# Reordering the turn between two steps of a graph layer on one NeuronCore: keys, laws, a guess, a product and a proof change places

## The chip, the cores and the metric

The kernel runs on one core of a Trainium2 chip. The metric is the device time of one execution, in microseconds (us). Five engines work side by side, each through its own queue in order: TensorE (PE; PEld is its weight load), VectorE (DVE), ScalarE (ACT), GpSimd (POOL), and SyncE (SP), which here only issues DMAs. GpSimd issues the indirect DMAs (gathers). "Clock" is the share of TensorE's full clock that was granted. The time before is 1377.8 us, the median of three runs (1377.0, 1377.8, 1383.6).

## The reference

Inputs are 3327 nodes with 256 features, a sparse weighted graph S, small weights, and a layer norm. With N = 3327 and two steps:

```python
def _top_p_attention(X, W1, W2, W3):
    q = X @ W1.T @ W2.T
    k = X @ W3.T
    probs = jax.nn.softmax(q @ k.T / TAU, axis=-1)
    ...
    keep_sorted = cs - sp < TOP_P          # cs: running sum of the sorted row
    ...
    A = probs * mask
    return A / jnp.maximum(A.sum(-1, keepdims=True), 1e-12)
R = S + jnp.eye(N); R = R / R.sum(-1, keepdims=True)
for n in range(STEPS):                      # 2
    A = _top_p_attention(Xa, W1, W2, W3)
    Xf = R @ Xf
    Xa = A @ Xa
    Z = Z + Xf @ U1[n].T + Xa @ U2[n].T
h = X + Z
return layernorm(h) * ln_g + ln_b           # and x + this, X = relu(layernorm(x))
```

So each step needs, for every node, a softmax row over all nodes, of which only the largest entries that hold 90% of the mass are kept, a product with the features, and a sparse graph product. The second step's attention reads the first step's result of all nodes.

## The kernel before, in words

Rows are cut into 26 tiles of 128 (tile 25 has 127 rows that count). The program is one function, `guess_graph_layer`; a slower exact search stands behind a branch and isn't run here.

For each tile and step the work is:

- **weights** (L581): project queries (L522), four chunks of logits on PE (L599) into two PSUM banks of the pool `ps_l`, each chunk taken out by ScalarE as an exponential with its sum (L603; the last chunk L607 and L609).
- **the guess** of the cut (L611 to L713): ScalarE sums up (L619 to L624), scans the row of 3328 values in passes called `ja` (L632), small VectorE instructions stand between the passes (L684, L685 after the second pass of the second step; L698 to L706 after the third), then POOL's (L675 to L711), then ScalarE's last one (L713). It needs the tile's "law", moments of its logits: `project` (L524, L531, L537, L540 to L544) for tiles 0 to 2, and `laws` (L548) for tiles 3 to 25 in the second step: eight groups on PE and VectorE (L556, L559 to L562), then two ScalarE and ten POOL instructions (L567 to L575) for all of them.
- **settle** (L722): VectorE masks the row (L728), takes the largest values (twenty L733, then L740 and L742 in turns, L747 to L752) and cuts the row (L762, or in two pieces L759 for the first and last tile). 
- **Sums** (L795): PE transposes the row (L808), ScalarE copies it out (L810), PE multiplies it with the features (L822); ScalarE scales the result in the first step (L831).
- **spread** (L1077): the graph product, six matmuls (L908, twelve records in the profile) of gathered rows, then an addition on VectorE (L1089, L1090), and in the first step a store to the table `vx`, from which the second step gathers (L900).
- **first_end** (L916, first step): transpose (L473, L476), two products (L921) with copies (L922, L924), and `prep` (L480): queries and keys of the second step (L484, copies L492 and L493). **finish** (L931) ends the second step.
- **prove** (L770): VectorE shows for a step that all guesses were good enough; `proof` (L954) runs it for the second step, and then a matmul (L958) makes a flag.

Between the steps stand `moments` (L503; L506, L508 to L512), the laws, and the first tiles' weights. The second step's first logits can only be made when the keys of tile 25 are there.

The pools `ps_a` (sums) and `ps_r` (graph products, `pz`) have one PSUM bank each, `ps_l` and `ps_t` (all else) two each.

The order on PE, ScalarE and VectorE, and on GpSimd from the second step on, is the order of the text (a chain of dependencies made at the end, L1193 and the lines below); only GpSimd's order before that, and SyncE's, is left to the tile framework. The text's order comes from strings: for each tile index i from -1 to 27 there are seven slots, and each letter of a slot's string advances one generator by a piece. `m` is the guess of tile i+1, `n` the one that was `m` before, `d` and `c` settle of tile i and of the one before, `s` spread, `w` and `q` weights, `e` first_end, `l` laws, `g` gathers, `f` finish, `v` proof. What a generator still holds at the end of the index is run there. `PLAN` is the usual string, `BEGIN`, `OPEN` and `LAST` those of the first and last indices. Before the change:

```python
    OPEN = {-1: ("llcmss", "lnms", "lwwnfd", "lcmdsssggggg", "fmgdswqdf", "llmdf", "lmwfdm"),
            0: ("cmssggg", "nms", "wwnfd", "cmdsss", "fdsmgwqdf", "mdf", "mwd"),
            1: ("cmss", "nms", "wwnfd", "cmdsssgggg", "fdsmwqdf", "mgdf", "mwdg")}
```

Of the kernel before, what the change touches and what calls it, by code (L numbers as in the profile page):

```python
# [9 lines left out]
F32 = mybir.dt.float32  # L10
# [8 lines left out]
P = 128  # L19
N = 3327  # L20
D = 256
DA = 64
NT = (N + P - 1) // P
# [321 lines left out]
def guess_graph_layer(ctx, tc, x, adj, w1t, w2t, w3t, u1t, u2t, ln_g, ln_b, out, flag):  # L345
# [17 lines left out]
    rows_of = lambda t: min(P, N - t * P)  # L363
# [431 lines left out]
    class Sums:  # L795
# [18 lines left out]
        def sum(self, g):  # L814

            t, k = divmod(g, PARTS)
            if k == 0:
                self.pa = ps_a.tile([P, 2 * D], F32, tag="pa", name="pa")[:, :D]
            eT = self.eT.pop(g)
            for c in range(4 * k, min(4 * k + 4, NT)):  # L820
                j = c % HALF * 2 + c // HALF
                PE.matmul(self.pa, eT[:, c - 4 * k, :], self.xa[:, j, :], start=c == 0, stop=c == NT - 1)  # L822
            if k < PARTS - 1:
                return None
            if self.step:
                return t, (self.pa, self.live.pop((self.step, t))["ra"])
            n = rows_of(t)
            dst = row.tile([P, D], F32, tag="xa", name="xa", bufs=2)
            if n < P:
                V.memset(dst, 0.0)  # L830
            S.activation(dst[:n], self.pa[:n], AF.Copy, scale=self.live.pop((self.step, t))["ra"][:n])  # L831
            return t, dst
# [83 lines left out]
    def first_end(t):  # L916
        aT = transposed(live.pop(("r", t)))
        yield
        pz = ps_r.tile([P, 2 * D], F32, tag="pr", name="pz")
        for c in range(ND):  # L920
            PE.matmul(pz, aT[:, c, :], u2[:, c].rearrange("p n d -> p (n d)"), start=c == 0, stop=c == ND - 1)  # L921
        S.copy(xw[:, t, :], pz[:, D:])  # L922
        sv = row.tile([P, D], F32, tag="sv", name="sv", bufs=2)
        S.copy(sv, pz[:, :D])  # L924
        G.tensor_tensor(sv, sv, x0[:, t, :], ALU.add)
        nc.sync.dma_start(sx[t], sv)
        yield
        yield from prep(aT, t)

# [24 lines left out]
    def proof():  # L954
        prove(1)
        yield
        pf = ps_t.tile([P, 4, P], F32, tag="pt", name="pf")
        PE.matmul(pf[:1, 0, :1], fl, ones, start=True, stop=True)  # L958
        V.tensor_copy(flag, pf[:1, 0, :1])
# [115 lines left out]


    def spread(step, t):  # L1077
        rr = rrs[:, t : t + 1]
# [17 lines left out]
    def refetch(t):  # L1096
        acs[t] = adjp.tile([P, KT, P], F32, tag="ac", name="ac", bufs=2)
        nc.sync.dma_start(acs[t].rearrange("p k r -> p (k r)"), cx[t])
        yield from fetched(vx, t, D)
# [13 lines left out]
             1: ("mdsssbba", "mcdsssbba", "edbawwbp", "msdbga", "mpdea", "dawwq", "emgq")}  # L1113
    OPEN = {-1: ("llcmss", "lnms", "lwwnfd", "lcmdsssggggg", "fmgdswqdf", "llmdf", "lmwfdm"),
            0: ("cmssggg", "nms", "wwnfd", "cmdsss", "fdsmgwqdf", "mdf", "mwd"),
            1: ("cmss", "nms", "wwnfd", "cmdsssgggg", "fdsmwqdf", "mgdf", "mwdg")}
    OPEN[2] = OPEN[3] = OPEN[1]
    fetching = itertools.chain(*(refetch(t) for t in range(NT)))
    LATE = (1, 4)
    BLOCKS = ({}, {1: (0, 1), 2: ()})  # L1120
# [4 lines left out]
    for step in range(2):  # L1125
        sums = Sums(step, live, xw if step else x0, AHEAD[step])

        for i in range(-1, NT + 2):
# [4 lines left out]
            if step == 1 and i == -1:  # L1133
                run(begun[0])
                prove(0)
                for e in es[4:]:
                    G.memset(e[:, N:NP], 0.0)
# [4 lines left out]
                m=measured(step, live[step, i + 1]) if valid(i + 1) else none,  # L1142
                s=spread(step, i - 2 + 2 * step) if valid(i - 2 + 2 * step) else none,
                w=later.pop((step, i + 2), none),
# [4 lines left out]
                b=none if step else product, q=none, v=proof() if step and i == NT else work.get("v", none),  # L1149
                l=laws(range(3, NT)) if step and i == -1 else work["l"] if step and i == 0 else none,  # L1150
            )
            if i >= 0 and valid(i + 3):
                later[step, i + 3] = weights(step, i + 3, live)
                work["q"] = itertools.islice(later[step, i + 3], 2 - step)
            if step == 0 and i >= NT - 2 and i < NT + 1:

                work["w"] = itertools.islice(begun[i - NT + 2], CUT - 1)
            if step == 0 and i >= NT - 3 and i < NT:
                work["q"] = itertools.islice(begun[i - NT + 3], 1)
            if i == -1:  # L1160
                work["w"] = begun[1] if step == 0 else itertools.chain(begun[1], begun[2])
            if step == 0 and i == 0:
                work["w"] = begun[2]
            for k in range(PARTS):
                g = PARTS * (i - 1) + k - LATE[step]
                summing = valid(g // PARTS)
                if step and valid((g + AHEAD[1]) // PARTS):
                    sums.turn(g + (k == 2), min(i, NT - 1))
                for c in ({**OPEN, **LAST} if step else BEGIN).get(i, PLAN[step])[k]:
                    next(work[c], None)  # L1170
# [12 lines left out]
            if step and i < 1:  # L1183
                next(fetching)
            for c in ("lcnwqsepb" if i > -1 else "cnwqsepb") if step else "cmwqsep" + "gb" * (i > 0):
# [55 lines left out]
```

## Time and profile before

| | |
|---|---|
| time, median of three runs | 1377.8 us (1377.0 to 1383.6) |
| the profiled execution | 1380.51 us, its span 1378.8 us |
| busy in the span | PE 1279.0 us (93%), DVE 1188.6 (86%), ACT 1079.2 (78%), POOL 954.0 (69%) |
| mean granted clock | 0.98 |
| last attention product of the first step ends | 772.6 us |
| first cut of the second step (L759) | 815.62 us |
| usual distance between two tiles in the second step | 21.0 us |
| last attention product of all ends | 1365.7 us |

The page cuts the span in 40 slices of 34.5 us; PE's row of busy tenths is 9 nearly all along, with a 7 and a 5 at about 760 to 830 us, the turn between the steps, and the clock's row is 6 and 9 there. Lines of the timeline give start, duration, engine, line of the kernel, operation, output and inputs, shapes, count, and in brackets the idle time before with what ended it. A matmul of 32-bit floats shows as two records. Ends of matmuls are modelled, and POOL's spans are rough.

### The profile page before, as it was taken

Reading aid. Unit: us, or ns where it says so; the run is one execution under the profiler, and the core shown is the slowest. Engines: PE = TensorE matmul, PEld = TensorE weight load, DVE = VectorE, ACT = ScalarE, POOL = GpSimd, SP = SyncE. Lnnn points to the kernel's source line nnn. Section 1 sums busy time; section 2 is a strip of 40 time slices with the busy share of each in tenths; the row PEclk is TensorE's granted clock in tenths of the full one; section 3 lists DMA queues with packets and bytes.
Section 4 is the critical chain, followed back from the end, with each engine's and each line's share of the span. In section 5 each row is a group of like instructions: output and inputs, shape, how many; then the busy total and the mean of one; then the engine's idle time right before and its main releaser. Section 6 shows DMA issues by size and latency. Waiting matters only on the chain.

```text
span 1378.8 us, 22108 instructions
## 1 busy us (share of the span) xinstructions
PE 1279.0 (93%) x6495; PEld 975.2 (71%) x6495; DVE 1188.6 (86%) x3637; ACT 1079.2 (78%) x2368; POOL 954.0 (69%) x1399
## 2 busy tenths in 40 slices
PE   5999999999999999999999759999999999999985
PEld 4535777776777777777777537777776777777774
DVE  6888889998898899999884389999998999999993
ACT  5466687787788788878774589899998999999941
POOL 6312888765777668766664377888888888888832
PEclk9999999999999999999999969999999999999998
DMA  8764454454454454444423112212222122221200
GB/s 275 246 183 146 123 152 132 132 148 117 123 152 121 126 147 115 150 136 128 140 66 98 50 58 62 81 62 88 62 81 79 60 89 62 81 88 50 89 23 23
DMA packets 92642, 149.77 MB, mean 109 GB/s; under 512 B 15425, under 2 KB 59072, under 8 KB 92512
## 3 DMA queue, kind: packets, MB, share of 16 engines
q1 hardware_dynamic: 75056, 105.37, 24.3%
q0 software_dynamic: 16640, 42.69, 12.0%
q8 instruction: 54, 0.88, 0.3%
q14 instruction: 76, 0.62, 0.1%
q10 hardware_dynamic: 816, 0.20, 0.1%
HBM read 120.93 MB, written 27.28 MB: 107 GB/s over the span
## 4 chain that ended last, share of the span: by engine, by line
PE 42%; DVE 26%; ACT 18%; POOL 7%; issue 4%; DMA 2%; SPq 0%; another core or an unknown queue 0%; ACTq 0%; DVEq 0%; POOLq 0%
PE pa L822 18%; ACT ja L632 7%; PE pt L808 5%; DVE w L728 5%; PE pr L908 5%; DVE cand L733 5%; PE pl L599 4%; DVE e L762 3%; PE pz L921 3%; ACT eT L810 2%; PE pz L989 2%; DVE bb L740 2%; DVE cand L742 2%; POOL xg L900 2%; ACT e L603 1%
## 5 line engine op out<-in xcount | busy, mean ns | idle before, releaser
L632 ACT ACTIVATE ja<-e,g 128x3328 uint8<-128x3328 f32 x106 | 325.7, 3073 | 0.1
L822 PE MATMUL pa<-xw,eT 128*128 128x256 f32 x1352 | 322.2, 383 | 3.3 <-DVE s L932 3.3
L822 PE MATMUL pa<-x,eT 128*128 128x256 f32 x1352 | 322.4, 380 | 0.0
L822 PEld LDWEIGHTS pa<-xw,eT 128*128 128x128 f32 x1352 | 249.9, 190 | 51.7 <-issue 14.4
L810 ACT COPY eT<-pt 128x512 f32<-128x512 f32 (+1 forms) x364 | 200.4, 558 | 89.1 <-PE pt L808 68.0
L822 PEld LDWEIGHTS pa<-x,eT 128*128 128x128 f32 x1352 | 242.9, 190 | 25.5
L733 DVE MAX8 cand<-w 128x8 f32<-128x168 f32 (+1 forms) x1040 | 253.4, 317 | 0.0
L900 POOL DMA_INDIRECT xg<-bx,index x130 | 166.7, 1282 | 51.7 <-issue 43.8
L808 PE MATMUL pt<-ident,e 128*128 128x128 f32 x1144 | 177.2, 278 | 18.8 <-DVE e L759 9.3
L808 PEld LDWEIGHTS pt<-ident,e 128*128 128x128 f32 x1144 | 140.1, 145 | 62.3 <-issue 35.6
L891 POOL DMA_INDIRECT ac<-in_adj,index x130 | 148.2, 1140 | 43.9 <-issue 29.4
L728 DVE SCALAR_TENSOR_TENSOR w<-e,g 128x3328 f32<-128x3328 f32 x44 | 162.1, 3684 | 2.7 <-ACT g L713 2.7
L900 POOL DMA_INDIRECT xg<-vx,index x130 | 133.4, 1026 | 34.1 <-issue 29.4
L908 PE MATMUL pr<-xg,ac 128*128 128x257 f32 (+1 forms) x520 | 142.7, 399 | 8.9 <-DVE s L1090 6.2
L762 DVE SCALAR_TENSOR_TENSOR e<-e,rec 128x3328 f32<-128x3328 f32 x40 | 147.9, 3697 | 0.6
L603 ACT ACTIVATE e<-pl 128x832 f32<-128x832 f32 x132 | 113.6, 864 | 17.7 <-PE pl L599 12.5
L908 PEld LDWEIGHTS pr<-xg,ac 128*128 128x128 f32 x520 | 95.0, 196 | 35.5 <-issue 14.8
L740 DVE MAX8 bb<-cand 128x8 f32<-128x160 f32 x286 | 92.6, 324 | 6.4
L599 PE MATMUL pl<-both,qT 64*128 64x416 f32 x416 | 92.1, 543 | 5.6 <-DVE e L995 2.4
L599 PE MATMUL pl<-after,qT 64*128 64x416 f32 x416 | 95.9, 555 | 0.5 <-ACT e L603 0.5
L844 DVE TENSOR_REDUCE fm<-at 128x4 f32<-128x512 f32 (+1 forms) x133 | 84.4, 635 | 11.8 <-DMA at<-in_adj 11.8
L676 POOL TENSOR_SCALAR g<-g 128x1 f32<-128x1 f32 x26 | 73.4, 2823 | 1.7
(260 smaller groups left out, 2156.9 us busy)
## 6 DMA issues: line engine op xcount, KB each, us to landing
at<-in_adj SPq DMA_DIRECT2D x114, 256.0 KB
cx<-ac SPq DMA_DIRECT2D x26, 384.0 KB
ac<-cx SPq DMA_DIRECT2D x26, 384.0 KB
wide<-in_adj SPq DMA_DIRECT2D x8, 832.0 KB
e<-in_adj SPq DMA_DIRECT2D x6, 832.0 KB
own<-bx SPq DMA_DIRECT2D x26, 128.5 KB
x<-in_x SPq DMA_DIRECT2D x13, 256.0 KB
s<-ax SPq DMA_DIRECT2D x26, 128.0 KB
```

What stands on the lines that cost most here:

```text
L599: PE.matmul(pl[:, a, :wd], qT[p, :], keys_of(step, a).rearrange("p a b -> p (a b)")[:, c : c + wd], start=True, stop=True)
L603: S.activation(e.rearrange("p (a n) -> p a n", a=2)[:, :, c : c + wd], pl[:, :, :wd], AF.Exp, accum_out=za[:, n : n + 1])
L632: S.activation(ja, e, f, bias=guess, scale=sign, accum_out=total)
L728: V.scalar_tensor_tensor(w, e, col(16), e, ALU.is_lt, ALU.mult, accum_out=d2)
L733: V.max(cand[:, 8 * s : 8 * s + 8], w[:, s * SEG : min(NP, (s + 1) * SEG)])
L762: V.scalar_tensor_tensor(e, e, at(1), e, ALU.is_ge, ALU.mult, accum_out=ra)
L808: PE.transpose(pt[:, j, :], e[:, (j0 + j) * P : (j0 + j + 1) * P], ident)
L810: S.copy(eT[:, :w, :], pt[:, :w, :])
L822: PE.matmul(self.pa, eT[:, c - 4 * k, :], self.xa[:, j, :], start=c == 0, stop=c == NT - 1)
L891: G.indirect_dma_start(out=ac[:, k, :], out_offset=None, in_=rows, in_offset=bass.IndirectOffsetOnAxis(ap=index[:, t, k : k + 1], axis=0), ...
L900: G.indirect_dma_start(out=xg[:, k, :w], out_offset=None, in_=rows, in_offset=bass.IndirectOffsetOnAxis(ap=index[:, t, k : k + 1], axis=0))
L908: PE.matmul(pr[:, :w], ac[:, k, :], own if k == KT - 1 else xg[:, k, :w], start=k == 0, stop=k == KT - 1)
```

## The change

It moves work in the turn between the steps, and little else:

1. The moments and the laws of tiles 0 to 2 (`foreseen`) are made at the start of tile 25's attention instead of after it.
2. The graph products of tiles 24 and 25 stand behind the end of the attention, one after the other.
3. For tile 25, `prep` (keys and queries) stands ahead of the products with U2; these go to the bank of `ps_a`, and VectorE copies them out instead of ScalarE. The zero fill of tile 25's scaled result is made when its sum starts.
4. Tile 2's logits are made in the second step, in slots of index 0, not beside tile 25's attention. Tile 1's last chunk follows tile 0's guess.
5. The laws of the other tiles (`y`) are spread over several slots: six groups before L684 of tile 0, two before L698, the POOL part at index 1.
6. The start of tile 1's settle and guess is shifted in the slots: L684 of tile 1 stands behind all twenty L733 of tile 0.
7. The graph product of tile 0 of the second step stands at the end of index 0, behind tile 2's logits and the queries of tile 3; its addition stands before L759 of tile 0.
8. One gather fewer is issued in the first two indices, so all later ones are one place behind; one more comes at the end.
9. The proof of the first step is made after that of the second, before the flag's matmul.

```diff
@@ class Sums, sum
             if k == 0:
                 self.pa = ps_a.tile([P, 2 * D], F32, tag="pa", name="pa")[:, :D]
+                if not self.step:
+                    self.dst = row.tile([P, D], F32, tag="xa", name="xa", bufs=2)
+                    if rows_of(t) < P:
+                        V.memset(self.dst, 0.0)
...
-            n = rows_of(t)
-            dst = row.tile([P, D], F32, tag="xa", name="xa", bufs=2)
-            if n < P:
-                V.memset(dst, 0.0)
+            n, dst = rows_of(t), self.dst
@@ def first_end(t)
         yield
-        pz = ps_r.tile([P, 2 * D], F32, tag="pr", name="pz")
+        if t == NT - 1:
+            yield from prep(aT, t)
+            yield
+        pool, tag = (ps_a, "pa") if t == NT - 1 else (ps_r, "pr")
+        pz = pool.tile([P, 2 * D], F32, tag=tag, name="pz")
...
-        S.copy(xw[:, t, :], pz[:, D:])
+        copy = V.tensor_copy if t == NT - 1 else S.copy
+        copy(xw[:, t, :], pz[:, D:])
...
-        S.copy(sv, pz[:, :D])
+        copy(sv, pz[:, :D])
...
-        yield
-        yield from prep(aT, t)
+        if t < NT - 1:
+            yield
+            yield from prep(aT, t)
@@ def proof()
         prove(1)
+        prove(0)
@@
+    def foreseen():
+        moments(1, gsum)
+        for t in range(3):
+            yield
+            early[t] = returned(project(1, t, queries=False))
+            if (1, t) in live:
+                live[1, t]["ms"] = early[t]
@@ the strings
+    END = {NT - 1: ("mdsss", "mcdsss", "edwwp", "msd", "mpde", "gdwwq", "emgql"),
+           NT: ("l", "cl", "el", "", "e", "", "e"),
+           NT + 1: ("", "yee", "sswyy", "yess", "yysss", "sssss", "")}
+    OPEN = {-1: ("cm", "nm", "nfd", "cmd", "fmsyyqdf", "mdf", "mwfdmggggg"),
+            0: ("cm", "nm", "nfd", "cmdgggg", "fddm", "mdwwf", "mwwqdssssss"),
+            1: ("cmss", "nms", "wwnfd", "ycmdsssgggg", "fdsmwqdf", "mgdf", "mwdg")}
+    OPEN[2] = OPEN[3] = ("cmss", "nms", "wwnfd", "cmdsssgggg", "fdsmwqdf", "mgdf", "mwdg")
+    lawing = laws(range(3, NT))
@@ the loop
-                prove(0)
...
-                s=spread(step, i - 2 + 2 * step) if valid(i - 2 + 2 * step) else none,
+                s=work["s"] if step and i == -1 else (itertools.chain(spread(0, NT - 2), spread(0, NT - 1)) if step == 0 and i == NT + 1 else
+                   spread(step, i - 2 + 2 * step) if valid(i - 2 + 2 * step) and (step or i < NT) else none),
...
-                l=laws(range(3, NT)) if step and i == -1 else work["l"] if step and i == 0 else none,
+                l=foreseen() if step == 0 and i == NT - 1 else work.get("l", none) if not step else none,
+                y=lawing,
...
-            if step == 0 and i >= NT - 2 and i < NT + 1:
+            if step == 0 and i == NT + 1:
+                work["w"] = begun[0]
+            if step == 1 and i == 0:
+                work["w"] = begun[2]
+            if step == 0 and i >= NT - 2 and i < NT:
                 work["w"] = itertools.islice(begun[i - NT + 2], CUT - 1)
...
-                work["w"] = begun[1] if step == 0 else itertools.chain(begun[1], begun[2])
+                work["w"] = begun[1]
...
-            if step == 0 and i == NT:
-                moments(1, gsum)
-                for t in range(3):
-                    live[1, t]["ms"] = returned(project(1, t, queries=False))
```

More of the change, by code (lines that the diff above doesn't have):

```diff
@@ L1113, in guess_graph_layer @@
              1: ("mdsssbba", "mcdsssbba", "edbawwbp", "msdbga", "mpdea", "dawwq", "emgq")}
[L1114 to L1117, printed above, removed]
+    END = {NT - 1: ("mdsss", "mcdsss", "edwwp", "msd", "mpde", "gdwwq", "emgql"),
[5 more added lines that the diff above has]
+    OPEN[2] = OPEN[3] = ("cmss", "nms", "wwnfd", "cmdsssgggg", "fdsmwqdf", "mgdf", "mwdg")
     fetching = itertools.chain(*(refetch(t) for t in range(NT)))
+    lawing = laws(range(3, NT))
     LATE = (1, 4)
@@ L1168, in guess_graph_layer @@
                     sums.turn(g + (k == 2), min(i, NT - 1))
-                for c in ({**OPEN, **LAST} if step else BEGIN).get(i, PLAN[step])[k]:
+                for c in ({**OPEN, **LAST} if step else {**BEGIN, **END}).get(i, PLAN[step])[k]:
                     next(work[c], None)
@@ L1184, in guess_graph_layer @@
                 next(fetching)
-            for c in ("lcnwqsepb" if i > -1 else "cnwqsepb") if step else "cmwqsep" + "gb" * (i > 0):
+            for c in ("ycnwqsepb" if i > 0 else "cnwqsepb") if step else ("cmwqsep" if i < NT + 1 else "cmwqep") + "gb" * (i > 0):
                 run(work[c])
-            if step == 0 and i == NT:
-                moments(1, gsum)
-                for t in range(3):
-                    live[1, t]["ms"] = returned(project(1, t, queries=False))
     run(work["f"])
```

## The prediction, made before the changed kernel had run

> **What bounds the kernel now.** I read first the busy shares by stretch (columns: stretch; length; then busy microseconds of PE, PEld, DVE, ACT, POOL; TensorE clock; DMA share; GB/s), then the timeline of each engine over 740 to 826 us, then the rhythm of the second step, then the tail. All times are on the clock of the profiled span.
>
> ```profile
> 744.40:772.70 28.30, 27.44 (x141) 21.43 (x141) 1.87 (x14) 9.52 (x24) 3.32 (x10) 1.00 0.17 53
> 772.70:798.10 25.40, 18.24 (x88) 13.18 (x86) 15.18 (x87) 18.62 (x41) 13.49 (x32) 0.80 0.25 68
> 798.10:815.60 17.50, 3.45 (x9) 2.18 (x8) 14.97 (x51) 15.21 (x31) 10.87 (x21) 0.70 0.23 67
> 870.00:960.00 90.00, 87.91 (x452) 67.96 (x451) 83.19 (x253) 83.78 (x162) 76.89 (x109) 1.00 0.27 82
> ```
>
> The end of the first step is PE's alone (27.4 of 28.3 us, DVE 1.9). Between the steps nobody is full: a serial chain ACT, DVE, POOL, ACT walks tile 0, then tile 1. From tile 2 on the second step turns in 21.0 us a tile (VectorE's L698 at 853.7, 874.7, 898.1, 919.1, 940.1), a loop of DVE and ACT with PE just behind it. So an earlier start of that loop is worth its full length at the end. The loop starts with the first L759; the lines around it:
>
> ```profile
> 771.73 1.02 PE L822 MATMUL pa<-x,eT 128*128 128x256 f32 x4
> ...
> 792.67 4.63 PE L908 MATMUL pr<-xg,ac 128*128 128x256 f32 x10
> 797.09 1.06 PE L908 MATMUL pr<-own,ac 128*128 128x256 f32 x2
> ...
> 817.06 1.94 PE L808 MATMUL pt<-ident,e 128*128 128x128 f32 x8 [9.28 <-DVE e L759]
> 818.93 3.14 PE L599 MATMUL pl<-after,qT 64*128 64x416 f32 x8
> ```
>
> ```profile
> 778.90 0.86 ACT L607 ACTIVATE e<-pl 128x830 f32<-128x830 f32 x1 [0.77 <-PE pq L556]
> ...
> 797.70 0.39 ACT L713 ACTIVATE g<-g 128x1 f32<-128x1 f32 x1 [0.91 <-POOL g L711]
> ```
>
> ```profile
> 768.59 0.16 DVE L510 COPY qm<-pq 128x1 f32<-128x1 f32 x1 [17.00 <-PE pq L508]
> ...
> 790.52 0.21 DVE L684 TENSOR_SCALAR g<-oa,g 128x1 f32<-128x1 f32 x1 [4.45 <-ACT ja L632]
> ...
> 795.18 0.27 DVE L698 TENSOR_SCALAR g<-oa,g 128x1 f32<-128x1 f32 x1 [0.29 <-ACT ja L632]
> ...
> 798.12 3.68 DVE L728 SCALAR_TENSOR_TENSOR w<-e,g 128x3328 f32<-128x3328 f32 x1 [1.97 <-ACT g L713]
> ...
> 804.33 0.47 DVE L1090 SCALAR_TENSOR_TENSOR s<-pr,rrs,s 128x256 f32<-128x256 f32 x1
> ...
> 815.62 1.28 DVE L759 SCALAR_TENSOR_TENSOR e<-e,rec 128x1024 f32<-128x1024 f32 x1
> ```
>
> To be seen: VectorE waits 17 us for L508 though its input was ready at 725.5; the last keys reach L607 6.3 us after the last attention product (772.6); the graph product of tile 0 (L908, 12 records) is done at 798.1, long before VectorE needs it at 804.33.
>
> **Part 1: attention's end without strangers (PE).** From 744.44 to the last L822 the old order has 28.2 us. Out of it go the graph products of tiles 24 and 25 before the last L822 (6+6 and 6 records: 1.30+1.30+1.30), the logits of tiles 2 and 1 (L599: 1.60 and 0.90), and the waits around L508/L524 with those matmuls (768.12 to 770.32, 2.2); L508 and three L524 come in (about 1.1), and two short waits for transpose banks, 0.4 and 0.3 (they share two PSUM banks with L808). So 28.2-8.6+1.8 = 21.4; adding up the new order itself by its pitches (0.44 for four L808, 1.73 for eight records of L822) gives 21.1, which I use: the last L822 ends at 765.5, 7.1 us earlier.
>
> **Part 2: last keys ahead of products.** Before, 772.6 to 778.9. Now: scale 0.47 (its zero fill was already made, 0.64 of waiting gone), transpose, copy, L484, key copy, two graph-product matmuls, one chunk of logits (0.97). L921 (1.72 and a wait of 0.65) is behind it. By the same rows: 765.7, 766.3, 766.7, 767.1, 767.8, 768.4, so L607 at 769.4: 9.5 us earlier.
>
> **Part 3: tile 0's guess.** L607 to L728 took 19.2 us. Two L607/L609 pairs of tiles 1 and 2 leave the middle (785.30 to 787.26, 2.0); tile 1's pair (1.0) now lies in the 0.9 wait for POOL before L713: no cost; without that wait it would cost 1.0. On VectorE, though, six law groups of 1.44, two copies of 0.42 (taken over from ScalarE) and the addition of tile 24 stand before L684, the addition of tile 25 and two more groups before L698. Walking them: group one 766.2; groups two to four from 769.9, bound by VectorE; copies to 775.0; groups to 777.9; tile 24 to 778.6; L684 at 779.15 when ScalarE's scan ends: nothing lost. Tile 25's product can start only when 778.6 frees the one product bank: 2.6 us at full clock, 781.3; addition 782.0; two groups to 784.6, against 783.8 where ScalarE is ready: 0.8 lost. L728 then at 769.4+19.2-2.0+0.1+0.8 = 787.5, 10.6 earlier.
>
> **Part 4: the new wait.** Old: L728 to L759 17.5 us. Moving L684 of tile 1 behind all twenty MAX8 removes its 1.8 wait, but L698 then waits about as much for ScalarE's third scan (both sets of scans keep their length), so 17.4 by VectorE alone. Before L759, however, now stands tile 0's addition (L1090 in old numbering), and its product has been put behind tile 2's logits. Those have two PSUM banks, freed by ScalarE's exponentials, which now stand after the third scan of tile 1. From L728 on, ScalarE's rows of tile 1: guess and two scans to +8.4, L684/L685 to +9.0, L686, L687 and the third scan to +13.0 (old: 8.4, 9.0, 13.1); then first exponential +13.95, logits chunk at half clock 1.57 (half of 3.14), again 1.57, L522 0.54: the product starts at +17.7. PE will have been idle for 13 us, so it is cold: twelve records cost 5.6 cold (4.63+1.06), 2.6 warm. The Trainium skill ("TensorE: Matmul & The Clock Gate", What's actually happening) says that one busy window of some 3.4 us releases the clock, and that the window runs freely. In this trace release took 6.6 us (791.5 to 798.1), 3.5 (804.85 to 808.4) and 5.0 (817.06 to 822.06). With the rule's shortest case the product takes 2.6 and ends at +20.3; with the longest seen 4.1, +21.8; I take the middle, 5.2 after the logits start: +21.1. With 0.2 latency and the addition's 0.48, L759 falls at +21.8 = 809.3. Queued behind the waiting addition on VectorE are L759, then tile 1's L728; PE waits for L759, so all stand still for 4.4 us. Gain left at L759: 815.62-809.3 = 6.3 us. From there VectorE's order to L684 of tile 2 is the old one (11.1 us), ScalarE is 1.7 ahead of need in spite of tile 2's four exponentials (4.1 us), which its order now holds here, so the 6.3 is handed on.
>
> **Part 5: laws, POOL and queues.** The last part of the laws (ten POOL instructions) moves between two of POOL's steps of tile 2. What it costs depends on VectorE:
>
> ```profile
> 815.60 4.22 POOL L570 TENSOR_SCALAR law<-law 128x23 f32<-128x23 f32 x4
> 819.90 3.61 POOL L571 TENSOR_TENSOR law<-law 128x23 f32<-128x23 f32 x1
> ...
> 878.69 3.54 POOL L709 TENSOR_TENSOR g<-g 128x1 f32<-128x1 f32 x1
> ```
>
> Free, such instructions take 0.19 to 0.32 (L572 to L575): 2.6 us together. Under a full-row VectorE instruction they wait for its end. The Trainium skill ("SBUF — State Buffer", SBUF: two separate sides) states the rule against this edit: VectorE with two SBUF inputs and GpSimd lock each other out for a whole instruction. By the free rows POOL is done 0.7 us before the next L762 (price 0); by the rule, one miss, and a miss is in the trace: L709 hit L762 at 878.7 and the tile took 23.4 instead of 21.0, price 2.4. I take 0, as nearest to the order worked out, and keep 2.4 for the range. POOL's gathers of tile 0 (six of 1.25 us) start after L711, about 787.3, and are 9 us ahead of their product; they need tile 25's rows in DRAM, stored from 782.1: no cost unless that takes over 5 us. SP's queue keeps its order except that stores and reloads of tiles 24 and 25 are later; the reloads are 25 us early. Fetches stand one behind the old count, still over a tile ahead.
>
> **Part 6: proof at the end.** The first proof leaves 774.70 to 778.4, where VectorE was waiting anyway: gain 0 there. At the end it follows the other:
>
> ```profile
> 1356.43 0.16 DVE L785 TENSOR_TENSOR fl<-fl,ok 127x1 f32<-127x1 f32 x1
> ...
> 1359.07 0.19 PE L958 MATMUL pf<-ones,fl 128*1 128x1 f32 x2
> ...
> 1361.24 4.48 PE L822 MATMUL pa<-xw,eT 128*128 128x256 f32 x20
> ```
>
> It takes 3.2 (its time without the last slow one) to 5 us (the first eleven took 3.7 here, next to POOL), so ends at 1359.8 to 1361.6, and L958 stands in PE's queue before the last attention products, which set the end. Loss 0.8 to 2.6; I take 1.5.
>
> **Sum.** 6.3-1.5 = 4.8. The profiled execution took 1380.5 (span 1378.8, 1.7 around it), 2.7 over the median; so 1375.7 on its own time, 1373.0 on the median of 1377.8.
>
> **Rivals.** *The head start is kept*: the product is out before VectorE comes, or one of POOL's misses goes. For it: L728 comes 10.6 earlier, and the profiled execution has two misses to lose. Against: ScalarE's order puts tile 2's exponentials after the third scan. 10.6-1.5 = 9.1, so 1368.7. *The clock falls once more or POOL misses once*: PE idles 3.2 us before tile 25's product (a gap of 3.1 at 1327.9 was enough to halve the clock), which then costs 2.9 more; or 2.4 for a miss. 4.8-2.7 leaves 2.1: 1375.7. *Slower*: POOL's place in the loop. In the quiet stretch POOL's last step of the guess (L711) ends at 922.74 and L762 starts about 0.2 us later. If the inserted laws and the later fetches push POOL over that edge, each missed tile costs 2.4; two use up the gain, from the third it is slower: 7.2-4.8, 1380.2. Against it: the misses before didn't repeat in the next tile.
>
> **Chances.** Mine 0.46 (a part of 0.10 below 1370.9); head start kept 0.32; one more loss 0.15; slower 0.07, of which 0.04 beyond 1384.7. About 0.5% (6.9 us) is what a measurement of this kernel can tell from no change. So faster 0.42, same 0.54, slower 0.04. The range leaves out the best third of the second case and most of the last: 1366.5 to 1377.5.
>
> **What would show it.** Right: last L822 of the first step near 765.5, L607 near 769.4, L728 near 787.5, a wait of about 4 us for the product before the first L759, L759 near 809, PE at clock 0.50 then; a wait of VectorE's second proof in PE's tail. Wrong: no such wait (then 1369), tile 25's product at half clock, a POOL instruction of over 3 us in tile 2's chain, or L698 turning in other than 21.0 us.

## The result, and the profile after

Over 20 runs each the changed kernel takes 1381.38 us (median; 1375.99 to 1384.8), the kernel before 1380.33. One of the latter's runs took 1880.39 us, which nothing here explains; all ratios in this document are of the fast runs and are not quotients of the medians. Here the ratio is 1.0004, 95% interval 0.9992 to 1.0017. No change that can be measured; 1373.0, a gain of 4.8 us, was predicted, and 1381.38 lies above the predicted range. (Over 20 runs the kernel before is 2.5 us slower than over the three that were known; that explains a part of the distance to 1373.0, not the missing gain.)

The profiled execution took 1379.58 us, span 1377.8. To compare it with the one before, a common mark is needed, for the first step, whose order is the same in both up to 744 us on the clock of the kernel before, strays by several us from run to run. I take the start of the last product with the lists (po<-lists). In the timeline of PE it stands here, before and after:

```profile
740.65 0.29 PE L876 MATMUL po<-lists,oh 128*128 128x13 f32 x2
```

```profile
736.74 0.29 PE L877 MATMUL po<-lists,oh 128*128 128x13 f32 x2
```

So the mark came 3.9 us earlier in the profile after, although nothing had changed in the order up to it. All times with a plus are counted from this mark; "the end" is the start of VectorE's last instruction, and the end of a matmul is taken as the start of the next one, as in the prediction. (After the change, lines are numbered higher: L822 is L826, L908 is L909, L1089 and L1090 are L1105 and L1106, L958 is L966, L900 is L901.)

| | predicted | before | after | gain |
|---|---|---|---|---|
| last attention product of the first step ends | +24.9 | +31.9 | +25.6 | 6.3 |
| last keys' exponential (first L607) | +28.8 | +38.3 | +29.9 | 8.3 |
| L728 of tile 0 | +46.9 | +57.5 | +50.0 | 7.4 |
| first cut, L759 of tile 0 | +68.7 | +75.0 | +74.3 | 0.7 |
| the end | | +628.6 | +631.6 | -3.0 |

Behind the mark the changed kernel is 3.0 us slower in these two executions, which the ratio of the whole runs doesn't show. VectorE's timeline after, around the first cut:

```profile
775.41 0.48 DVE L1106 SCALAR_TENSOR_TENSOR s<-pr,rrs,s 128x256 f32<-128x256 f32 x1
...
780.56 0.17 DVE L1105 RECIPROCAL rrs<-pr 128x1 f32<-128x1 f32 x1 [3.62 <-PE pr L909]
...
783.82 0.27 DVE L698 TENSOR_SCALAR g<-oa,g 128x1 f32<-128x1 f32 x1
...
786.78 3.69 DVE L728 SCALAR_TENSOR_TENSOR w<-e,g 128x3328 f32<-128x3328 f32 x1 [1.99 <-ACT g L713]
...
798.91 0.21 DVE L684 TENSOR_SCALAR g<-oa,g 128x1 f32<-128x1 f32 x1 [3.52 <-POOL g L677]
...
810.63 0.48 DVE L1106 SCALAR_TENSOR_TENSOR s<-pr,rrs,s 128x256 f32<-128x256 f32 x1 [2.68 <-PE pr L909]
811.03 1.28 DVE L759 SCALAR_TENSOR_TENSOR e<-e,rec 128x1024 f32<-128x1024 f32 x1
```

Three waits are to be seen, and each has its line on another engine. The first is for tile 25's product (3.62), then the law groups run, and L698 of tile 0 comes when they are done. PE after, with the windows of 1 us beside it (columns as in the prediction; the clock is the column after POOL's):

```profile
775.99 3.84 PE L909 MATMUL pr<-xg,ac 128*128 128x257 f32 x10 [2.11 <-issue]
```

```profile
774.00:775.00 1.00, 0.00 (x0) 0.00 (x0) 0.93 (x5) 1.00 (x1) 0.23 (x1) 1.00 0.36 107
...
778.00:779.00 1.00, 1.00 (x4) 0.81 (x3) 0.00 (x0) 1.00 (x1) 0.80 (x4) 0.50 0.00 0
```

PE stood for 2.11 us, until VectorE's L1106 of tile 24 (775.41, 0.48 long) had emptied the one product bank; VectorE came to it only behind two law groups. Then the clock fell to 0.50, and tile 25's product took 4.5 us and not 2.6. The second wait is for GpSimd, whose timeline shows why. Before the change, one gather stood ahead of tile 1's L675:

```profile
797.82 1.09 POOL L900 DMA_INDIRECT xg<-vx,index  x1 [0.16 <-issue]
800.39 1.63 POOL L675 TENSOR_SCALAR g<-g,ms 128x1 f32<-128x1 f32 x1 [1.48 <-ACT g L674]
```

After it:

```profile
786.92 4.55 POOL L901 DMA_INDIRECT xg<-vx,index  x1 [0.60 <-issue]
...
796.78 0.95 POOL L901 DMA_INDIRECT xg<-vx,index  x1 [0.30 <-issue]
797.77 0.34 POOL L675 TENSOR_SCALAR g<-g,ms 128x1 f32<-128x1 f32 x1
```

Tile 1's L675 has all that it needs at 788.95 (ScalarE's L674) and runs at 797.77, behind six gathers. The first of them starts under VectorE's L728, takes 4.55 us and ends 1.0 us after L728 does (790.47); the others take 0.95, with 0.30 between. The Trainium skill ("DMA: Bandwidth & Descriptors", SWDGE vs HWDGE vs iDMA) says that GpSimd writes the rings of its DMAs to SBUF, and that VectorE locks it out there in its 2-port perf modes. The trace shows the wait for L728's end; it doesn't show in which mode L728 ran, so that this is the reason is not shown. The third wait, 2.68 us, is the one foreseen, for tile 0's product. And the end, PE after:

```profile
1356.44 0.19 PE L966 MATMUL pf<-ones,fl 128*1 128x1 f32 x2 [2.12 <-DVE fl L791]
1356.56 3.31 PE L826 MATMUL pa<-xw,eT 128*128 128x256 f32 x8
...
1360.09 4.68 PE L826 MATMUL pa<-xw,eT 128*128 128x256 f32 x20
```

```profile
1358.00:1359.00 1.00, 1.00 (x4) 0.81 (x3) 0.00 (x0) 0.00 (x0) 0.00 (x0) 0.50 0.06 16
```

The flag's product waits 2.12 us for the second proof, and the products behind it run at half clock for 3.5 us (3.31 in place of 1.99). From L759 of tile 25 to the end it is 26.7 us; before, 22.9.

### The profile page after: what moved, and what is told of

The parts are those of the page before. It is cut to its first block, busy times and chain, and to the rows that moved or that the text cites. A ratio compares the mean times of both kernels' runs of the same rounds, so it can differ in the third digit from the quotient of the medians.

```text
span 1377.8 us, 22106 instructions
## 1 busy us (share of the span) xinstructions
PE 1275.6 (93%) x6495; PEld 973.3 (71%) x6495; DVE 1191.1 (86%) x3639; ACT 1081.4 (78%) x2366; POOL 962.4 (70%) x1399
## 4 chain that ended last, share of the span: by engine, by line
PE 44%; DVE 29%; ACT 16%; issue 4%; POOL 3%; DMA 1%; SPq 0%; ACTq 0%; DVEq 0%; POOLq 0%
PE pa L826 19%; ACT ja L632 7%; DVE w L728 6%; PE pt L808 6%; PE pr L909 5%; DVE cand L733 5%; PE pl L599 5%; DVE e L762 4%; PE pz L926 3%; ACT eT L810 2%; DVE x L762 2%; DVE bb L740 2%; DVE cand L742 2%; PE pz L997 1%; ACT e L603 1%
## 5 line engine op out<-in xcount | busy, mean ns | idle before, releaser
L826 PE MATMUL pa<-xw,eT 128*128 128x256 f32 x1352 | 325.4, 386 | 3.3 <-DVE s L939 3.3
L826 PE MATMUL pa<-x,eT 128*128 128x256 f32 x1352 | 322.4, 380 | 0.0
L826 PEld LDWEIGHTS pa<-xw,eT 128*128 128x128 f32 x1352 | 252.0, 191 | 52.5 <-issue 14.4
L826 PEld LDWEIGHTS pa<-x,eT 128*128 128x128 f32 x1352 | 243.3, 191 | 25.6
L733 DVE MAX8 cand<-w 128x8 f32<-128x168 f32 (+1 forms) x1040 | 253.5, 319 | 0.0
L901 POOL DMA_INDIRECT xg<-bx,index x130 | 162.8, 1252 | 51.2 <-issue 43.8
L808 PE MATMUL pt<-ident,e 128*128 128x128 f32 x1144 | 176.8, 277 | 10.8 <-DVE e L762 3.4
L808 PEld LDWEIGHTS pt<-ident,e 128*128 128x128 f32 x1144 | 139.5, 144 | 53.9 <-issue 23.9
L728 DVE SCALAR_TENSOR_TENSOR w<-e,g 128x3328 f32<-128x3328 f32 x44 | 161.9, 3680 | 2.7 <-ACT g L713 2.7
L901 POOL DMA_INDIRECT xg<-vx,index x130 | 137.1, 1055 | 36.3 <-issue 30.1
L762 DVE SCALAR_TENSOR_TENSOR e<-e,rec 128x3328 f32<-128x3328 f32 x40 | 147.7, 3693 | 0.6
L909 PE MATMUL pr<-xg,ac 128*128 128x257 f32 (+1 forms) x520 | 140.7, 394 | 5.4 <-DMA xg<-bx,index 2.7
L909 PEld LDWEIGHTS pr<-xg,ac 128*128 128x128 f32 x520 | 93.4, 193 | 31.5 <-issue 16.7
L931 POOL TENSOR_TENSOR sv<-sv,x 128x256 f32<-128x256 f32 x26 | 27.7, 1066 | 72.4 <-ACT sv L930 56.5
```

Of the source, the lines that this page charges most:

```text
L728: V.scalar_tensor_tensor(w, e, col(16), e, ALU.is_lt, ALU.mult, accum_out=d2)
L733: V.max(cand[:, 8 * s : 8 * s + 8], w[:, s * SEG : min(NP, (s + 1) * SEG)])
L762: V.scalar_tensor_tensor(e, e, at(1), e, ALU.is_ge, ALU.mult, accum_out=ra)
L808: PE.transpose(pt[:, j, :], e[:, (j0 + j) * P : (j0 + j + 1) * P], ident)
L901: G.indirect_dma_start(out=xg[:, k, :w], out_offset=None, in_=rows, in_offset=bass.IndirectOffsetOnAxis(ap=index[:, t, k : k + 1], axis=0))
L909: PE.matmul(pr[:, :w], ac[:, k, :], own if k == KT - 1 else xg[:, k, :w], start=k == 0, stop=k == KT - 1)
```

## The experiments

The theory: the start is earlier by 8 us, and is lost (a) in the cold product of tile 25, (b) at the six gathers, (c) at the product of tile 0 behind tile 2's logits, (d) at the flag. The rival: the order of the turn is limited elsewhere, and these waits only change places. All ratios are to the kernel before on the same chip, with 95% intervals. The chips differ: the mark lies between +715 and +748 us of the span. The two measures at the right are not the same: "end" is one execution, with its luck of the clock behind the mark, and the ratio comes from 8 to 22 executions of the changed version and has the first step in it. They differ by up to 4 us (flag_last: 0.7 us slower than before by the end, 3.3 faster by the ratio), so a difference of 2 or 3 us needs both. Behind the mark (L698 of tile 1 is left out):

| run | L728 (0) | L759 (0) | L698 (2) | end | ratio |
|---|---|---|---|---|---|
| before | +57.5 | +75.0 | +92.0 | +628.6 | |
| before_again | +57.5 | +75.0 | +92.1 | +628.8 | 1.0007 (0.9994 to 1.0020) |
| before_proof_end | +57.5 | +75.0 | +92.4 | +632.7 | 1.0035 (1.0021 to 1.0049) |
| after | +50.0 | +74.3 | +91.4 | +631.6 | 1.0004 (0.9992 to 1.0017) |
| after_again | +50.0 | +75.4 | +92.5 | +631.4 | 1.0006 (0.9993 to 1.0019) |
| flag_last | +50.0 | +75.6 | +92.7 | +629.3 | 0.9976 (0.9964 to 0.9989) |
| proof_back | +50.0 | +75.6 | +92.7 | +629.5 | 0.9999 (0.9982 to 1.0016) |
| law_after | +48.4 | +72.6 | +89.6 | +626.1 | 1.0003 (0.9983 to 1.0023) |
| gathers_later | +50.0 | +72.0 | +89.1 | +628.1 | 0.9990 (0.9978 to 1.0001) |
| product_first | +48.3 | +69.8 | +87.4 | +626.2 | 0.9991 (0.9981 to 1.0001) |
| best | +48.4 | +65.7 | +89.8 | +624.0 | 0.9978 (0.9964 to 0.9991) |
| best2 | +48.5 | +65.8 | +90.8 | +625.9 | 0.9970 (0.9957 to 0.9983) |
| best3 | +48.5 | +66.5 | +93.1 | +627.6 | 1.0006 (0.9992 to 1.0020) |
| best5 | +48.4 | +65.7 | +91.3 | +627.3 | 0.9978 (0.9962 to 0.9994) |
| best4 | +48.4 | +66.4 | +90.3 | +625.8 | 0.9984 (0.9967 to 1.0001) |
| three | +48.4 | +69.9 | +87.5 | +621.2 | 0.9945 (0.9927 to 0.9962) |

**The end: flag_last, proof_back, before_proof_end.**

```diff
-            NT + 1: ("fv", "f", "", "", "f", "f", "f")}
+            NT + 1: ("f", "f", "", "", "f", "f", "fv")}
```

> The changed kernel, but the product that makes the flag (L966 and the copy L967) stands behind the last matmul of the sum and not two blocks before it; both proofs stay at the end. Theory A (TensorE's wait for the second proof ate the gain): the 2.12 us idle before L966 goes, no cold clock follows (L826 x8 1.9 us in place of 3.31), the last L939 comes 3.8 us earlier at the same first L759 (811.0 -> end near 1374.0 span, median 1377.6). Rival B (the end is bound by something else, for instance the output's store or the reading of the flag, so that a later flag lengthens the tail by as much): span stays within 1 us of 1377.8, median 1381.

Measured: no idle time before L966, which now stands behind the last L826, and 22.5 us from L759 of tile 25 to the end:

```profile
1340.83 2.97 PE L826 MATMUL pa<-xw,eT 128*128 128x256 f32 x13
1343.73 0.19 PE L966 MATMUL pf<-ones,fl 128*1 128x1 f32 x2
```

From the first L759 to the end it is 553.7 us, in the profile after 557.3; behind the mark only 2.3 us are gained, since L759 came 1.3 later here. The ratio, 0.9976, is 0.28% below that of the changed kernel, 3.8 us. Theory A.

```diff
@@ proof()
-        prove(0)
@@ the loop, step 1, i == -1
                 run(begun[0])
+                prove(0)
```

> The changed kernel with tile 24's, that is buffer 0's, proof put back between the steps (before the guess of tile 0), as it was before the change. Theory A: the tail is as before the change (no wait before the flag's product, -3.8 us), and between the steps the proof fills a VectorE gap: L684 of tile 0 is 3.1 us later, but L698 of tile 0 only 0.4 us, since six of eight law groups stand between them; net -3.4, span near 1374.4, median 1378.0. Rival B (every VectorE microsecond in the turn is on the path): first L759 3.7 us later, net 0, median 1381.

L684 of tile 0 came 2.4 us later, L698 at the same +47.1, the end as in flag_last: behind the mark theory A. The ratio of the whole doesn't show it (0.9999); its profiled first step was 3.6 us longer than that of flag_last, and no step here explains that.

> The kernel before with one part of the change only: the proof of buffer 0 goes from between the steps to the end, right behind the other. Theory A (at the end it holds up the flag's product, TensorE stands about 2.1 us and then runs cold for 1.6 us more; between the steps it stood beside other work and frees nothing): behind the mark 628.6 + 3.7 = 632.3 us, ratio 1.0027. Rival B (as predicted, only the wait of 1.5 us, no cold clock): 630.1, ratio 1.0011. Rival C (it frees VectorE between the steps): 628.6 or less, ratio 1.000.

This moves `prove(0)` to the end of the kernel before. Up to L759 nothing changes (+75.0), so between the steps the proof had cost nothing, and 4.1 us are lost behind it: theory A. In all six profiles with the proof ahead of the flag PE stands for 2.11 to 2.13 us; in three of them the clock then fell and the end took 26.7 us from L759 (after, before_proof_end, product_first), in three it held and took 25.0. One of the latter, after_again:

```profile
1364.45 0.19 PE L966 MATMUL pf<-ones,fl 128*1 128x1 f32 x2 [2.11 <-DVE fl L791]
1364.57 1.99 PE L826 MATMUL pa<-xw,eT 128*128 128x256 f32 x8
```

The wait is sure, the cold clock chance. It costs 2.2 us or 3.9.

**The turn: law_after, gathers_later, product_first.**

```diff
@@ END, NT + 1
-"yess", "yysss", "sssss", ""
+"yess", "sssyy", "sssss", ""
```

> The changed kernel with tile 24's product and its VectorE part ahead of two of the law groups in the last turn of the first step, not behind them. Theory A (TensorE's stop of 2.11 us ahead of tile 25's product waits for VectorE to empty the one buffer that tile 24's product fills, and VectorE is at a law group; the stop lets the clock fall to 0.5, tile 25's product takes 4.7 in place of 3.0 us, and the last two law groups queue behind it, ahead of L698 of tile 0): the stop shrinks to under 1 us, L698 of tile 0 at mark + 45.1 in place of 47.1, first L759 2 us earlier, behind the mark 629.6, ratio to the changed kernel 0.9985. Rival B (ScalarE's third pass, not the law groups, holds L698): no change at L698 and behind the mark.

PE's stop shrank to 0.82 us, and tile 25's product kept the clock:

```profile
781.84 0.67 PE L909 MATMUL pr<-xg,ac 128*128 128x257 f32 x2 [0.82 <-PE pr L909]
782.44 1.27 PE L556 MATMUL pq<-qm,both 64*128 64x130 f32 x12
783.64 2.00 PE L909 MATMUL pr<-xg,ac 128*128 128x257 f32 x8
```

L698 of tile 0 came at +45.5, where ScalarE's scan now ends last (1.18 us of waiting for it): 1.6 earlier, L759 1.7 to 2.9 earlier than in the two profiles of the changed kernel. Theory A. At the end it is 5.3 us ahead of after_again, 2.9 of them at L759 and 2.4 between the first and the last cut. Of the latter, 2.0 lie between L698 and L759 of tile 25, where PE stops until VectorE's L762 is done; after_again, then law_after:

```profile
1332.85 1.94 PE L808 MATMUL pt<-ident,e 128*128 128x128 f32 x8 [3.13 <-DVE e L762]
```

```profile
1331.60 1.06 PE L808 MATMUL pt<-ident,e 128*128 128x128 f32 x8 [1.82 <-DVE e L762]
```

Behind the long stop the clock is 0.50 for about 6 us, behind the short one it stays at 1.00. So 2.0 us of the difference come from a third place where the clock counts, far from the turn; why the stop was shorter here is open. The ratio of law_after, with its wide interval, shows none of the 5.3 us.

```diff
@@ OPEN
-    -1: (..., "mdf", "mwfdmggggg"), 0: ("cm", "nm", "nfd", "cmdgggg", "fddm", "mdwwf", "mwwqdssssss")
+    -1: (..., "mdf", "mwfdm"), 0: ("cmggg", "nm", "nfd", "cmd", "fddm", "mdggwwf", "mwwqdssssssgggg")
```

> The changed kernel with one gather in place of six ahead of tile 1's guess in GpSimd's order (1, guess, 3, guess, 2, guess, 5). Theory A (tile 1's guess waits for GpSimd, not for VectorE): L684 of tile 1 at 795.4 in place of 798.9, all behind it 3.5 us earlier, first L759 at 807.5, kept: span 1374.3, median 1377.9. Rival B (tile 0's product then waits for its last gather): first L759 not before 809.5, median 1380.

L684 of tile 1 came at +58.5 in place of +62.1, without a wait, and L759 at +72.0, 3.6 us earlier than in flag_last on the same chip, 2.3 earlier than in after:

```profile
773.55 0.20 DVE L684 TENSOR_SCALAR g<-oa,g 128x1 f32<-128x1 f32 x1
...
786.61 0.48 DVE L1106 SCALAR_TENSOR_TENSOR s<-pr,rrs,s 128x256 f32<-128x256 f32 x1 [4.59 <-PE pr L909]
787.01 1.28 DVE L759 SCALAR_TENSOR_TENSOR e<-e,rec 128x1024 f32<-128x1024 f32 x1
```

Theory A for what held up tile 1's guess, and as far as L698 of tile 2. But VectorE now waits 4.59 us for tile 0's product, and L759 lies between the two forecasts (+70.8 and +72.8).

```diff
-"mdwwf", "mwwqdssssss"
+"mdsssssswwf", "mwwqd"
```

> The changed kernel with the first product of the second step (L909 of tile 0) ahead of tile 2's logits in TensorE's order. Theory A (the product's place is what VectorE waits for, 2.68 us at 807.95): the wait goes, first L759 at 808.4 to 808.8, 2.3 to 2.7 us earlier than 811.03, kept to the end: span 1375.3, median 1379.0. Rival B (the gathers of tile 0 land after the logits could run, so that the product in front delays logits and guess of tile 2): L759 earlier but L698 of tile 2 not (828.1), no gain, median 1381.

L759 stands right behind L752 and the addition, without a wait, at +69.8, 5.9 us earlier than in flag_last:

```profile
792.37 0.20 DVE L752 TENSOR_REDUCE rec<-cum 128x1 f32<-128x48 f32 x1
792.49 0.48 DVE L1106 SCALAR_TENSOR_TENSOR s<-pr,rrs,s 128x256 f32<-128x256 f32 x1
792.88 1.28 DVE L759 SCALAR_TENSOR_TENSOR e<-e,rec 128x1024 f32<-128x1024 f32 x1
```

Of the 5.9 us, 1.7 are tile 25's product, whose clock held in this profile after the same 2.11 us; the rest, 4.2, is more than the 2.3 to 2.7 expected, because in flag_last the product of tile 0 was partly at half clock (4.1 us, in after 2.9) and VectorE had waited for it for 4.1. Theory A.

**The changed kernel and the kernel before once more.**

> The changed kernel once more, unaltered. Counted from a mark that both kernels share (the start of the last product with the lists, po<-lists, in the first step) the profiled execution before takes 628.6 us to the start of VectorE's last instruction and the changed one 631.6, so 3.0 us more, while the medians differ by 0.04%. Theory A (the first step's length is chance from run to run, and the changed kernel is slower by what happens behind the mark): 631.6 +- 1.5 again behind the mark, ratio to before 1.002. Rival B (the changed kernel's first step is itself 2 to 3 us shorter): ratio 1.000 again, and the mark earlier than in the kernel before on the same chip.

+631.4 again, as theory A has it, with other parts: a colder product of tile 0 (L759 1.1 us later) and a longer cold stretch at tile 25 (1.2), but the clock held at the flag. The ratio, 1.0006, is the same as at first, as rival B has it; A's 1.002 lies just outside its interval. The mark came at 743.2, and at 748.4 in before_proof_end on the same chip, but at 745.3 and 746.5 in law_after and best, which have the changed kernel's order up to the mark. So rival B is neither shown nor ruled out.

> The kernel before, unaltered, against itself. Theory A (what differs from profile to profile is the first step, whose order is the same in all these kernels; behind the mark the kernel repeats to a few tenths): 628.6 +- 0.5 us behind the mark, the mark anywhere within 4 us of the changed kernels' on the same chip, ratio within 0.0013 of 1. Rival B (behind the mark it varies by 2 us or more, like the kernels with a stop of 2.1 us after which the clock sometimes falls): 626.5 or 630.5.

The kernel before repeats to 0.2 us behind the mark, and its ratio to itself is 1.0007: theory A. The changed kernel's two ratios can't be told from this one.

**Together: best, best2, best3, best5, best4, three.** The first has all four moves.

> Four of the moves on the changed kernel together: the flag's product last, the gathers behind tile 1's guess, the first product ahead of tile 2's logits, tile 24's product ahead of two law groups. Theory A (they are one chain and add up): L698 of tile 0 at mark + 45.1, first L759 at mark + 65.3 (before 75.0, changed 74.3), then the same 553.7 us as in the run with the flag last; behind the mark 619.0 us, ratio to before 0.993. Rival B (the gains overlap, since the guess of tile 2 or the first product's gathers set the start once tile 1's guess is early): first L759 at mark + 69, behind the mark 623, ratio 0.9955.

L759 at +65.7, as theory A has it. But of 9.2 us gained on the kernel before, L698 of tile 2 keeps 2.2. VectorE in that run:

```profile
812.24 1.27 DVE L759 SCALAR_TENSOR_TENSOR e<-e,rec 128x1024 f32<-128x1024 f32 x1
...
820.55 3.68 DVE L728 SCALAR_TENSOR_TENSOR w<-e,g 128x3328 f32<-128x3328 f32 x1 [4.10 <-ACT g L713]
...
836.32 0.27 DVE L698 TENSOR_SCALAR g<-oa,g 128x1 f32<-128x1 f32 x1 [0.79 <-ACT ja L632]
```

That is rival B's overlap (624.0 and 0.9978 for its 623 and 0.9955), though at tile 2 and not at L759. The next four try to free what stands in front of tile 2: one gather forward (index 0 `"cmgggg"`, `"mdgsssssswwf"`); with it ScalarE's first exponential of tile 2 ahead of the third scan (`"fddmw"`); and tile 1's product behind tile 0's transposes in each of the two (index 1 `"cm"`, `"nm"`, `"wwnfdss"`, `"ycmdssgggg"`, `"fdmwqdssf"`, `"mgdsf"`).

> The four moves once more, with tile 0's fifth gather ahead of GpSimd's L688 of tile 1 and only one gather behind L691. In the run of the four moves L759 came at mark + 65.7, but VectorE's L728 of tile 1 only at mark + 74.05, 4.1 us after VectorE was free, since the first product waited for its fifth gather (issued at mark + 61.2, landed at + 63.0) with tile 2's logits and ScalarE's L713 of tile 1 behind it. Theory A: the fifth gather is issued 2 us earlier, the product ends at mark + 62.5, L713 of tile 1 comes at mark + 70.8 and L728 at + 71.2; behind the mark 621.1 us (four moves 624.0, before 628.6), ratio to before 0.9955. Rival B (TensorE is then late with tile 0's transposes, which stand behind three matmuls of tile 1's product and its gathers, and the loop is no earlier): 624, ratio 0.998.

> As the run before, and ScalarE takes out tile 2's first chunk of logits (L603, 0.86 us) ahead of the third scan of tile 1 and not behind it, so that the second chunk can be multiplied ahead of the first product. Theory A (the logits of tile 2 set L713 of tile 1): L698 of tile 1 and L759 are 0.85 later (L759 at mark + 66.6), but L713 of tile 1 comes at + 69.5 to 70.5 and L728 at + 70.7; behind the mark 620.7. Rival B (ScalarE's third scan sets everything behind it): all is 0.85 later than in the run before.

> The run with the fifth gather forward, and at index 1 tile 1's product goes behind tile 0's first transposes (L808), its VectorE addition from ahead of L684 of tile 2 to ahead of L698. There L808 of tile 0 waited for tile 1's gathers 8 us after L759 had ended, ScalarE's copies stood behind it and with them tile 2's second scan, so that L698 of tile 2 came at mark + 90.8, 18 us after L728 of tile 1 (13 elsewhere). Theory A: L698 of tile 2 at mark + 86, behind the mark 621 us (625.9 before this move, 628.6 in the kernel before the change), ratio to before 0.9945. Rival B (tile 2's guess is set by ScalarE's logits of tile 3 or by GpSimd, which ends its gathers late): L698 of tile 2 not before + 89.5, behind the mark 625.

> The same move of tile 1's product on the run that also has tile 2's first exponential ahead of tile 1's third scan. There L728 of tile 1 came at mark + 71.2 and L698 of tile 2 at + 93.1, since TensorE stood in tile 1's product until + 78.5 with tile 0's transposes behind it. Theory A: L698 of tile 2 at mark + 84 to 85, behind the mark 619 us, ratio to before 0.9925. Rival B (as in the run beside it): L698 of tile 2 not before + 89.5, behind the mark 624.

L728 of tile 1 came earlier (+72.8, +71.2, +72.3, +71.5 against +74.05), L698 of tile 2 in none of them: each time rival B. In best5 PE waited for a gather of tile 1 whose issue lay under VectorE's L728 (813.82 to 817.5) and took 3.87 us:

```profile
814.46 3.87 POOL L901 DMA_INDIRECT xg<-vx,index  x1 [0.30 <-issue]
```

```profile
820.49 1.22 PE L909 MATMUL pr<-xg,ac 128*128 128x256 f32 x2 [3.75 <-DVE cand L733]
```

(L733 is only the last event before it; it writes nothing that this product reads.) Tile 0's next transposes (L808) stood behind it, and behind them ScalarE's copy and tile 2's third scan. The moved gathers themselves seemed to take back the gain. So the last run leaves them where the change had put them, and has flag_last, law_after and product_first together:

> The changed kernel with three of the moves: the flag's product last, the first product ahead of tile 2's logits, tile 24's product ahead of two law groups. GpSimd's gathers stay as the change put them (six ahead of tile 1's guess). Theory A (moving gathers behind tile 1's guess only shifts them into the lock of VectorE's L759 and L728 and in front of tile 1's product and tile 2's guess, so that it brings nothing behind tile 2): L759 at mark + 69.7, L698 of tile 2 at mark + 87.4, earlier than in the runs of the four moves (89.8 to 93.1), behind the mark 622.0 us, ratio to before 0.995. Rival B (the late start of tile 1's guess costs its 3.5 us to the end): behind the mark 626 or more, ratio 0.998.

All as theory A had it: L759 later than in best, L698 of tile 2 at +87.5, 2.3 us earlier, +621.2 behind the mark and the ratio 0.9945: 7.4 us behind the mark, 7.6 by the ratio. Its interval lies below those of the kernel before against itself and of the changed kernel, so it is faster than both. Of the 7.4 us, 4.5 are there at L698 of tile 2, 2.0 come in the loop, and 0.9 from L698 of tile 25 on, where the clock held. At L698 of tile 2 product_first alone was as early (+87.4), with luck at tile 25's product, whose clock held; of the 5.0 us that `three` adds to it at the end, 4.2 are the flag's. That the two measures agree so closely is partly luck, too. Between the first cut and L698 of tile 2 VectorE waits only for ScalarE's scans, 0.78 us before L698:

```profile
811.86 1.28 DVE L759 SCALAR_TENSOR_TENSOR e<-e,rec 128x1024 f32<-128x1024 f32 x1
...
816.01 3.67 DVE L728 SCALAR_TENSOR_TENSOR w<-e,g 128x3328 f32<-128x3328 f32 x1
...
829.50 0.28 DVE L698 TENSOR_SCALAR g<-oa,g 128x1 f32<-128x1 f32 x1 [0.78 <-ACT ja L632]
```

## Why the prediction was wrong

It was right in its first half and in the direction of each cost that it counted, and wrong in the sum: 6.3 us of gain at L759 were 0.7 (-0.4 in after_again), and the loss of 1.5 at the end was 3.9 (2.2). One cost was put at nothing (part 5), two were too small (parts 3 and 6).

- **Parts 1 and 2** (attention's end, last keys) held: +25.6 for +24.9, +29.9 for +28.8, 1.2 us late together.
- **Part 3** had tile 25's product "2.6 us at full clock". The bank came free 1.3 us later than reckoned, and the 2.1 us that PE stood were enough for the clock to fall; it took 4.5. That is the mishap named among the rivals, at 2.9. In the profiles it is the rule, five of the six with that stop. L698 came 3.1 us late and L728 3.2. law_after shows that the law groups ahead of tile 24's addition cause the stop.
- **Part 5 is the step that failed by its reasoning.** It says that POOL's gathers of tile 0 "are 9 us ahead of their product", and puts them at "no cost". The sentence looks at who waits for the gathers, and not at what is queued behind them. That was tile 1's L675 to L677, and with them L684, the third scan and tile 2's exponentials. From L728 to L752 it took 21.0 us; before, and in the sum, 17.3: 3.7 lost. gathers_later gives 3.6 back at L684 of tile 1 and, against flag_last, at L759. Of the 3.7, 2.4 show at L759, since the sum had a wait for the product there anyway. The first gather's 4.55 us under L728 was not in the sum either (1.25 was), though the rule that VectorE shuts GpSimd out was weighed a few lines above, for the laws only.
- **Part 4** (the new wait) held as a mechanism: a wait of 2.68 us (after), 4.1 (flag_last), for 4.4 predicted; the product ended 23.8 us behind L728 for 21.1, since its logits started later. product_first takes the wait away.
- **The laws at index 1** cost nothing. Two POOL instructions of over 3 us do stand in tile 2's chain, the sign that was called wrong: L675 (3.30) and L677 (3.76) of the guess, under VectorE's L759 and L728. But before the change two of the laws stood at that place (L570 and L571, 4.22 and 3.61), and from L759 to L698 of tile 2 it is 17.1 us after as before. The loop handed the start on: from L698 of tile 2 to that of tile 25, 488.9 us, before 489.4. The rival on the slow side, GpSimd's knife-edge, did not happen.
- **Part 6** had the mechanism and missed the size: a wait of 2.12 for a loss of 1.5, and the cold clock behind it (1.7) was not in the sum.

The working: 6.3 - 3.2 (L728) - 2.4 (from L728 to L759) = 0.7; 0.7 - 3.9 + 0.2 (loop) = -3.0. The ratios of the changed kernel show a loss of 0.6 to 0.8 us only, with intervals that end at 2.3 and 2.6. The distance to 3.0 may be the clock's luck at its three places, or a first step that is shorter in the changed kernel; that isn't settled. The kernel before against itself shows 0.07%, so in whole runs no difference is seen.

Open, too, is what exactly sets tile 2 once tile 1's guess is early: that best to best4 lose it and three doesn't is measured, and that GpSimd's gathers under VectorE's long instructions are the common cause is read from timelines, of which only best5's is shown here.

## What to carry to other kernels

When a step is put into an in-order queue, ask two things: who waits for it, and what is queued behind it; a transfer issue with no one waiting for it can still hold up the next tile's guess. A product that needs only a small flag belongs behind the last long work of its engine, not in front of it. And a gain at the head of a pipeline has to be followed to the point where the loop repeats (here tile 2): the version with the earliest first cut was not the fastest.

## What the hardware showed that was not expected

PE's stops of 2.1 us let the clock fall to 0.50 in some executions and not in others, at the same place of the same code: three of six at the flag, five of six before tile 25's product. Each fall there cost about 1.7 us. Two more places fit in: PE's stop for the L762 ahead of tile 25's transposes, near the end, and one in the first step, at about 67 us, where the clock was left at 1.00 by four stops of 2.8 us. Counted over the profiles of this case:

| PE's stop | place | clock fell |
|---|---|---|
| 3.11 to 3.15 us | L762 | 11 of 11 |
| 2.80 to 2.82 us | first step | 11 of 15 |
| 2.16 to 2.18 us | L762 | 3 of 3 |
| 2.11 to 2.13 us | flag, tile 25's product | 8 of 12 |
| 1.82 and 1.45 us | L762 | 0 of 2 |
| 0.82 and 0.83 us | tile 25's product | 0 of 7 |

The Trainium skill ("TensorE: Matmul & The Clock Gate", What's actually happening) puts the fall behind an idle window of about 3.4 us, and says that the window runs freely. The second half would fit a clock that falls by chance; the first does not fit, since 2.1 us were often enough here.
